# The first gather table made from the inputs, and the last wave's way back in three pieces with ScalarE and GpSimd

## The chip, the cores and the metric

The kernel runs on one core of a Trainium2 chip. Its time is device microseconds of one execution; the number that counts is the median of several. Times in the text are microseconds (us) unless marked ns. The engines are TensorE (PE, with its weight loads as PEld), VectorE (DVE), ScalarE (ACT), GpSimd (POOL) and SyncE (SP, which here only issues DMAs).

## What is computed

The input is a graph of 6250 nodes with 256 features and 106250 directed edges, sorted by target. One call runs two layers, each with graph sums, an attention without a softmax over pairs, and a feed-forward part:

```
xn = layernorm(x)
x  = x + gnn0(xn) + mix0(xn)          # two rounds of neighbour sums; linear attention
x  = x + ffn0(layernorm(x))           # each node goes to the one best of 8 experts
xn = layernorm(x)
x  = x + gnn1(xn) + mix1(xn)          # one round of neighbour sums
x  = x + ffn1(layernorm(x))           # 4 experts, top 2, and a shared part
```

A round of `gnn0` is `x + relu(D A D (x W) + b)`, where A is the adjacency and D the diagonal of 1/sqrt(deg) (`dinv` in the kernel). `gnn1` uses the mean over neighbours (`rdeg` is 1/max(deg, 1)).

## The kernel before

The nodes lie in 49 tiles of 128 rows, and `xa` holds all of them on chip as 128 x 49 x 256 fp32. The edges lie in 831 chunks of 128. A neighbour sum reads, for each chunk, 128 rows of a table in DRAM by an indirect DMA that GpSimd issues (L562), builds a 0/1 matrix of targets on VectorE (L566), and multiplies the two on TensorE into PSUM (L585). There are three such sums, with three tables: `t1` (fp32), `t2` and `t3` (each as fp32 and as three bf16 parts that add up to it; the sums read the parts). The stages in order:

1. Preparation: load the edges and `x`; count the degrees on TensorE (L414 to L435); the statistics of the first layer norm by `ln_stats` (L233, L234), `rstd` (square root on ScalarE L238, reciprocal on VectorE L239); the norm in place in `xa` on ScalarE (L469, groups of seven tiles); then `first_table` (L324): `dinv`, each tile times `dinv` alternately on ScalarE (L334) and VectorE (L336) into `t1s`, and a store of four tiles at a time into `t1` (L337).
2. The first sum over `t1`, and beside it the linear attention of `mix0` (`columns0`, L688: transposes of `xa`, then products), which settles tile by tile into `xa` and the table `t2`.
3. The second sum over `t2`; beside it the router of `ffn0` (`route`) sends nodes to slots of experts, and `serve` (L1056) takes slots in chunks of 128: 16 hidden products with Gelu on ScalarE (L915, L917), then the chosen expert's product (L1103). The nodes are two waves, tiles 0 to 35 and 36 to 48. When a wave is served, `back` (L1151) brings its rows home in pieces of two tiles.
4. The third sum over `t3` and beside it the attention and feed-forward of the second layer.

`back` of one piece: load `yb` (L1156); on VectorE add it to `xa` (L1160) and take statistics; square root on ScalarE; on VectorE the norm `xn` (L242); then `split` (L299) into three bf16 parts: a cast on ScalarE (L301), a subtraction on VectorE (L302), a cast (L303), a subtraction (L304); then both stores, `t3f` (L1172) and `t3b` (L1173). All first-wave pieces run while the second wave is served; the second wave's seven pieces (six of two tiles, one of one) run when no expert work is left, and the third sum needs all of `t3`.

What runs beside what is written by a planner, `pace` (L613). A job is a generator: each step issues instructions and yields the TensorE time it took and the time until its next step may go. `kinds` is a list of job sources by priority with the most that may live at once. In the stages of the sums the order of TensorE, SyncE and GpSimd is the order in which the planner issued; VectorE and ScalarE are ordered by the framework's scheduler. `later` puts an issue at a given time ahead in the planner's clock.

The lines that the change turns on:

```python
for T in range(t0, t0 + n):                                   # L469, in the preparation
    nc.scalar.activation(xa[:, T, :], xa[:, T, :], AF.Identity, bias=shift[...], scale=rs0[:, T:T + 1])
...
(lambda: backs, lambda: back(*backs.pop(0)), 2),              # two pieces alive at most
...
yield 0.0, 4.0 * n                                            # in back, between the work and the stores
```

Of the kernel before, what the change touches and what calls it, by code (L numbers as in the profile page):

```python
# [107 lines left out]
BT = 2  # L108
# [40 lines left out]
def gps_kernel(ctx: ExitStack, tc: tile.TileContext, i: dict, out: bass.AP):  # L149
# [73 lines left out]
    rdeg = consts.tile([P, NT], F32, name="rdeg")  # L223
    mv0 = consts.tile([P, NT, 2], F32, name="mv0")
    rs0 = consts.tile([P, NT], F32, name="rs0")
    mv1 = consts.tile([P, NT, 2], F32, name="mv1")
    rs1 = consts.tile([P, NT], F32, name="rs1")
    mv2 = consts.tile([P, NT, 2], F32, name="mv2")
# [67 lines left out]

    ov = dram.tile([NPAD, C], F32, name="ov")

    def split(dst, row, res):  # L299

        nc.scalar.copy(dst[:, :C], row)  # L301
        nc.vector.tensor_sub(res, row, dst[:, :C])  # L302
        nc.scalar.copy(dst[:, C:2 * C], res)  # L303
        nc.vector.tensor_sub(dst[:, 2 * C:], res, dst[:, C:2 * C])  # L304

    xa = nodes.tile([P, NT, C], F32, name="xa")
    sp = edges.tile([P, NCHP], I32, name="sp")
# [13 lines left out]

    gflag = consts.tile([1, 1], I32, name="gflag")

    def first_table(tp):  # L324

        sd = small.tile([P, NT], F32, name="sdeg")
        nc.scalar.activation(sd, deg, AF.Sqrt, bias=ones[:, 0:1], scale=1.0)
        nc.vector.reciprocal(dinv, sd)
        for t0, n in groups(4):
            ts = tp.tile([P, 4, C], F32, name="t1s", bufs=3)  # L330
            for t in range(n):
                T = t0 + t
                if t % 2:
                    nc.scalar.activation(ts[:, t, :], xa[:, T, :], AF.Copy, scale=dinv[:, T:T + 1])  # L334
                else:
                    nc.vector.tensor_scalar(ts[:, t, :], xa[:, T, :], dinv[:, T:T + 1], None, op0=ALU.mult)  # L336
            nc.sync.dma_start(tiles_of(t1[0], t0, n), ts[:, :n, :])  # L337
        dmx = small.tile([P, NT], F32, name="dmax")
        nc.vector.tensor_scalar(dmx, deg, 1.0, None, op0=ALU.max)
        nc.vector.reciprocal(rdeg, dmx)  # L340

    with ExitStack() as st:
        prep = pool(st, "prep")
# [114 lines left out]
        nc.vector.tensor_scalar(gpen, gpen, 1.0e6, None, op0=ALU.mult)  # L458
        nc.vector.tensor_scalar(lof, lof, gpen, None, op0=ALU.subtract)

        for t0, n in groups(7):
            for T in range(t0, t0 + n):
                ln_stats(mv0[:, T, :], xa[:, T, :])
            rstd(rs0[:, t0:t0 + n], mv0[:, t0:t0 + n, 1], n)
            shift = small.tile([P, 7], F32, name="shift")
            nc.vector.scalar_tensor_tensor(shift[:, :n], mv0[:, t0:t0 + n, 0], -1.0, rs0[:, t0:t0 + n],
                                           op0=ALU.mult, op1=ALU.mult)
            for T in range(t0, t0 + n):
                nc.scalar.activation(xa[:, T, :], xa[:, T, :], AF.Identity, bias=shift[:, T - t0:T - t0 + 1],  # L469
                                     scale=rs0[:, T:T + 1])  # L470
        first_table(pool(st, "table0"))

    general = nc.values_load(gflag[0:1, 0:1], min_val=0, max_val=1,
                             skip_runtime_bounds_check_because="it is the result of a comparison")
# [1 line left out]
    with tc.If(general):  # L476
        with ExitStack() as st:
            gw_ = pool(st, "gdeg")
            nc.vector.memset(deg, 0.0)
            hi = gw_.tile([P, NCHP], I32, name="g_hi")  # L480
            nc.vector.tensor_scalar(hi, dsti, 7, None, op0=ALU.arith_shift_right)
            hif = gw_.tile([P, NCHP], F32, name="g_hif")
            nc.vector.tensor_copy(hif, hi)
            nc.vector.tensor_scalar(hi, dsti, P - 1, None, op0=ALU.bitwise_and)
            low = gw_.tile([P, NCHP], F32, name="g_low")
            nc.vector.tensor_copy(low, hi)
            with tc.For_i(0, NCH, 1) as c:
# [10 lines left out]
                nc.vector.tensor_add(deg, deg, gd)  # L498
        with ExitStack() as st:
            first_table(pool(st, "table1"))  # L500

# [111 lines left out]
    def pace(kinds, slot, factor=1.0):  # L613

        now = [0.0]
        live = []

        def step():  # L620
            for k, (waiting, begin, most) in enumerate(kinds):
                while sum(j[1] == k for j in live) < most and waiting():
# [12 lines left out]

        def later(us, do):

            def once():
                do()
                yield from ()  # L640

            live.append([now[0] + us, None, once()])

        def due():

            for k, (waiting, begin, most) in enumerate(kinds):
                if sum(j[1] == k for j in live) < most and waiting():
# [12 lines left out]

        return step, other, rest, now, later
# [26 lines left out]
    def columns0():  # L688

        for gi, (t0, n) in enumerate(gs):  # L690
            transposed(xnt[:, :, t0 * P:(t0 + n) * P], lambda t: xa[:, t0 + t, :], n, "xtr", vs)
# [459 lines left out]
    def back(v, t0, n):  # L1151

        r = rows_of(t0 + n - 1)
        yb = work.tile([P, BT, C], F32, name="yb")
        y0 = 1 + (t0 - WAVES[v][0]) * P
        nc.sync.dma_start(yb[:r, :n, :], ys[v][y0:y0 + (n - 1) * P + r, :].rearrange("(t p) c -> p t c", p=r))  # L1156
# [7 lines left out]
        xn = work.tile([P, BT, C], F32, name="xn2")  # L1164
        ts = work.tile([P, BT, 3 * C], BF16, name="t3s")
        for t in range(n):
            T = t0 + t
            normalize(xn[:, t, :], xa[:, T, :], mv2[:, T, :], rs2[:, T:T + 1])
            res = work.tile([P, C], F32, name="res3")
            split(ts[:, t, :], xn[:, t, :], res)  # L1170
        yield 0.0, 4.0 * n
        nc.sync.dma_start(tiles_of(t3[0], t0, n), xn[:, :n, :])  # L1172
        nc.sync.dma_start(tiles_of(t3[1], t0, n), ts[:, :n, :])  # L1173

    def back_groups(v):

# [3 lines left out]
            yield v, t0, n  # L1180
            t0 += n

    routing, backs, finished = [], [], []

    filled = [v == len(WAVES) - 1 for v in range(len(WAVES))]
    waves, routed = list(range(len(WAVES))), [0]
# [30 lines left out]
    def serves():  # L1217
# [4 lines left out]
        if not filled[v]:  # L1222
# [1 line left out]
        finished.append(v)  # L1224

    step, other, rest, _, later = pace([(lambda: summed, lambda: settles(settle2), 1),
                                 (lambda: backs, lambda: back(*backs.pop(0)), 2),
                                 (lambda: routing, routes, 1),
                                 (lambda: waves and routed[0] > WAVES[waves[0]][0] + BEHIND, serves, 1)],
                                  1.25 * (NCH + NT + sum(map(chunks_of, range(len(WAVES))))) / NCH, factor=1.1)  # L1230
    with tc.manual_schedule(engines=ORDERED):
        neighbour_sums(t2, 1, gq, after2, True, other, depth=3)
        lag[:] = 1.0, 0.0
    gq_stack.close()
    for v in range(len(WAVES)):
# [444 lines left out]
```

## Time and profile before

| | |
|---|---|
| median of 3 runs | 3787.47 us (3784.19 to 3789.47) |
| the profiled execution | 3793.69 us, its span 3791.5 us |
| busy share of the span | PE 83%, PEld 68%, DVE 37%, ACT 26%, POOL 67% |
| first sum, first to last gather | 98.96 to 1173.88 us |
| second sum, first gather | 1192.12 us |
| last expert product ends | 2579.18 us |
| third sum, first gather | 2633.69 us |

An entry of a view names the source line, the engine, the operation, the tile written and the tile read, and the count; for a timeline the first two columns are start and length, and a bracket behind it says how long the engine had been idle and what ended that. A "waits" row reads: who waited, for what, us in total, times, longest. The framework's source lines of helpers (`ln_stats`, `rstd`, `split`) are shared by all callers, so tiles tell them apart.

### The profile page before, as it was taken

To read this page: it belongs to the slowest core of one execution; us is meant where nothing else is said; L and a number is where in the kernel's file an instruction comes from. 1 tells how busy PE (TensorE), PEld (TensorE's weight loads), DVE (VectorE), ACT (ScalarE), POOL (GpSimd) and SP (SyncE) were. 2 spreads that over 40 slices of the span, in tenths; PEclk is the share of its full clock that TensorE was granted. 3 is DMA by queue.
4 is the path that set the end of the run, shared out by engine and by line. 5 is a ranking of instruction groups with operands and counts; after the bars stand their busy time and mean duration, and the time that the engine had idled before them with its cause. 6 is when DMAs were issued, how large, how long until landed. Compare 5 with 4: busy or idle time off the path is not lost. (4 is left out here: it accounts for less than half of the span.)

```text
span 3791.5 us, 59772 instructions
## 1 busy us (share of the span) xinstructions
PE 3162.1 (83%) x23151; PEld 2579.1 (68%) x23151; DVE 1394.0 (37%) x5166; ACT 972.5 (26%) x2011; POOL 2536.0 (67%) x2657
## 2 busy tenths in 40 slices
PE   3788888878886778888888799873899999999998
PEld 2578777767774555666666576662788887778887
DVE  6222322222222223333333333563544445444444
ACT  4111100000000222333333242551123323233333
POOL 0777777777776777777777677312777777777772
PEclk9989866666665778999999899886999999999999
DMA  4566544444444556666666676585555555555552
GB/s 151 145 181 181 150 130 134 128 134 129 130 133 138 159 158 208 203 198 199 202 204 211 183 251 197 184 260 165 152 158 158 156 157 156 154 152 156 155 157 68
DMA packets 330381, 628.08 MB, mean 166 GB/s; under 512 B 56986, under 2 KB 219589, under 8 KB 330080
## 3 DMA queue, kind: packets, MB, share of 16 engines
q0 software_dynamic: 151488, 449.62, 40.8%
q1 hardware_dynamic: 177742, 174.07, 15.0%
q8 instruction: 184, 3.01, 0.3%
q14 instruction: 117, 0.96, 0.1%
q10 hardware_dynamic: 850, 0.43, 0.0%
HBM read 549.15 MB, written 74.75 MB: 165 GB/s over the span
## 5 line engine op out<-in xcount | busy, mean ns | idle before, releaser
L562 POOL DMA_INDIRECT rows<-t1f,sp x831 | 806.5, 971 | 358.4 <-issue 240.0
L562 POOL DMA_INDIRECT parts<-t3b,sp x831 | 808.4, 973 | 289.0 <-issue 214.2
L562 POOL DMA_INDIRECT parts<-t2b,sp x831 | 800.5, 963 | 290.0 <-issue 221.9
L585 PEld LDWEIGHTS <-parts 128*128 128x128 bf16 x9972 | 562.8, 103 | 432.3 <-DMA parts<-t2b,sp 209.0
L585 PE MATMUL sums<-onehotf,rows 128*128 128x84 f32 (+1 forms) x3324 | 660.9, 350 | 226.4 <-DMA rows<-t1f,sp 166.3
L585 PEld LDWEIGHTS sums<-onehotf,rows 128*128 128x128 f32 x3324 | 596.3, 255 | 321.5 <-DMA rows<-t1f,sp 224.6
L585 PE MATMUL sums<-onehot,parts 128*128 128x84 bf16 (+2 forms) x9972 | 659.9, 210 | 178.8 <-DMA parts<-t2b,sp 159.3
L915 PE MATMUL hid<-ft,fw 128*128 128x256 f32 (+1 forms) x1696 | 467.9, 411 | 21.3 <-DVE ft L275 8.6
L566 DVE TENSOR_TENSOR onehot<-iota_w,lof 128x336 bf16<-128x336 bf16 x416 | 209.6, 505 | 544.0 <-PE sums L585 483.5
L915 PEld LDWEIGHTS hid<-ft,fw 128*128 128x128 f32 x1696 | 311.2, 201 | 72.5 <-DVE ft L275 15.0
L566 DVE TENSOR_TENSOR onehotf<-iota_wf,lof 128x336 f32<-128x336 f32 x208 | 105.8, 509 | 548.3 <-PE sums L585 543.6
L917 ACT ACTIVATE ht<-hid,fb 128x256 f32<-128x256 f32 (+1 forms) x424 | 195.6, 472 | 259.1 <-PE hid L915 254.3
L1103 PE MATMUL exp<-wd,ht 128*128 128x256 f32 x896 | 229.6, 391 | 3.4 <-DMA wd<-in_L_ffn_Wd 3.1
L605 ACT COPY aggt<-sums 128x88 f32<-128x88 f32 x96 | 22.3, 232 | 737.5 <-PE sums L585 731.8
L1103 PEld LDWEIGHTS exp<-wd,ht 128*128 128x128 f32 x896 | 160.7, 192 | 21.2 <-DMA wd<-in_L_ffn_Wd 3.5
L1493 PE MATMUL fc_ps<-ht,fc 128*128 128x256 f32 (+1 forms) x600 | 160.6, 391 | 0.0
L1505 PE MATMUL fc_ps<-fc,ut 128*128 128x256 f32 x588 | 157.4, 393 | 0.0
L1075 POOL DMA_INDIRECT ys<-y,fs x56 | 56.7, 1012 | 134.4 <-DVE y L1108 64.4
L788 PE MATMUL h<-w,aggt 128*128 128x256 f32 x392 | 145.0, 507 | 0.3 <-DVE aggt L606 0.3
L936 PE MATMUL gate<-ht,wg 128*8 128x256 f32 (+1 forms) x400 | 112.5, 415 | 0.9 <-ACT ht L917 0.9
L1493 PEld LDWEIGHTS fc_ps<-ht,fc 128*128 128x128 f32 x600 | 105.0, 192 | 9.8
L1505 PEld LDWEIGHTS fc_ps<-fc,ut 128*128 128x128 f32 x588 | 102.9, 191 | 9.3
(358 smaller groups left out, 4145.1 us busy)
## 6 DMA issues: line engine op xcount, KB each, us to landing
wd<-in_L_ffn_Wd SPq DMA_DIRECT2D x56, 1024.0 KB
xs<-zero SPq DMA_DIRECT2D x8, 1799.0 KB
rows<-t1f,sp POOLq DMA_INDIRECT x831
parts<-t2b,sp POOLq DMA_INDIRECT x831
parts<-t3b,sp POOLq DMA_INDIRECT x831
t2b<-t2s SPq DMA_DIRECT2D x49, 192.0 KB
t3b<-t3s SPq DMA_DIRECT2D x24, 384.0 KB
fs<-xs SPq DMA_DIRECT2D x56, 128.5 KB
```

Source lines behind the costliest of these rows:

```text
L562: nc.gpsimd.indirect_dma_start(out=gs[:, j, :], out_offset=None, in_=(table if f32 else parts)[:, :], in_offset=bass.IndirectOffsetOnAxis( ...
L566: nc.vector.tensor_tensor(ohs[:, :n, :], (iota_wf if f32 else iota_w)[:, None, :WIN].to_broadcast([P, n, WIN]), lof[:, c:c + n, None].to_b ...
L585: nc.tensor.matmul(ps[b][:, h, n0 - b * P:n1 - b * P], lhsT=g[:, k * C + h * P:k * C + (h + 1) * P], rhs=oh[:, n0 - w0:n1 - w0], start=Fal ...
L605: nc.scalar.copy(dst[:, :, WIN:], sums[:, :, WIN:P])
L788: nc.tensor.matmul(h, lhsT=at[:, k, :], rhs=w[:, k, :], start=(k == 0), stop=(k == 1))
L915: nc.tensor.matmul(h_ps[:, :w], lhsT=fw1[:, k, m * P:(m + 1) * P], rhs=ft[:, k, :w], start=(k == 0), stop=(k == 1))
L917: nc.scalar.activation(ht[:, m, :w], h_ps[:, :w], AF.Gelu, bias=fb1[:, m:m + 1], scale=1.0)
L936: nc.tensor.matmul(lt, lhsT=wg[:, m, :], rhs=ht[:, m, :w], start=(m == 0), stop=(m == 7))
L1075: nc.gpsimd.indirect_dma_start(out=ys[v][:, :], out_offset=bass.IndirectOffsetOnAxis(ap=to, axis=0), in_=y, in_offset=None)
L1103: nc.tensor.matmul(y_ps, lhsT=ht[:, m, q * P:(q + 1) * P], rhs=wd[:, m, :], start=(m == 0), stop=(m == 7))
L1493: nc.tensor.matmul(u_ps[:, :w], lhsT=fc1[:, k, m * P:(m + 1) * P], rhs=ht[:, k, :w], start=(k == 0), stop=(k == 1))
L1505: nc.tensor.matmul(h_ps, lhsT=ut[:, m, t * P:(t + 1) * P], rhs=fc2[:, m, :], start=False, stop=(m == 5))
```

## The change

It has three parts.

The first table is made straight from the inputs. `dinv` and `rdeg` are taken in `factors`, as soon as the degrees are there. For groups of five tiles the norm's scale and shift are multiplied by `dinv` on VectorE (`by`), one ScalarE instruction per tile writes the table piece from the raw `xa`, and five tiles are stored at once. `xa` itself is normalised in place later, as a step of `columns0` in the first sum, on ScalarE, with a wait of 3 us in the planner's clock before the transposes. (The old form of `first_table` stays for a branch that these inputs do not take.)

The last wave's way back: up to three pieces alive (the bound of a kind may now be a function), the norm on ScalarE with a shift worked out on VectorE, the last subtraction of `split` on GpSimd. The first wave's pieces: one alive at a time. In both, a piece's job ends when its work is issued, and the stores are put `later`, 4 us per tile on in the planner's clock.

The tiles of `back` move from the pool `work` (two buffers) to a pool of their own, `backs` (three buffers), on the other side of the memory.

```diff
+    def factors():
         sd = small.tile([P, NT], F32, name="sdeg")
         nc.scalar.activation(sd, deg, AF.Sqrt, bias=ones[:, 0:1], scale=1.0)
         nc.vector.reciprocal(dinv, sd)
+        dmx = small.tile([P, NT], F32, name="dmax")
+        nc.vector.tensor_scalar(dmx, deg, 1.0, None, op0=ALU.max)
+        nc.vector.reciprocal(rdeg, dmx)
...
-        for t0, n in groups(7):
+        factors()
+        tp = pool(st, "table0")
+        for t0, n in groups(5):
             for T in range(t0, t0 + n):
                 ln_stats(mv0[:, T, :], xa[:, T, :])
...
-            for T in range(t0, t0 + n):
-                nc.scalar.activation(xa[:, T, :], xa[:, T, :], AF.Identity, bias=shift[:, T - t0:T - t0 + 1],
-                                     scale=rs0[:, T:T + 1])
-        first_table(pool(st, "table0"))
+            by = small.tile([P, 2, 5], F32, name="by", bufs=3)
+            nc.vector.tensor_mul(by[:, 0, :n], rs0[:, g], dinv[:, g])
+            nc.vector.tensor_mul(by[:, 1, :n], shift[:, g], dinv[:, g])
+            ts = tp.tile([P, 5, C], F32, name="t1s", bufs=3)
+            for t in range(n):
+                nc.scalar.activation(ts[:, t, :], xa[:, t0 + t, :], AF.Identity, bias=by[:, 1, t:t + 1],
+                                     scale=by[:, 0, t:t + 1])
+            nc.sync.dma_start(tiles_of(t1[0], t0, n), ts[:, :n, :])
...
     def columns0():
         for gi, (t0, n) in enumerate(gs):
+            for T in range(t0, t0 + n):
+                nc.scalar.activation(xa[:, T, :], xa[:, T, :], AF.Identity, bias=shift[:, T:T + 1],
+                                     scale=rs0[:, T:T + 1])
+            yield 0.0, 3.0
             transposed(xnt[:, :, t0 * P:(t0 + n) * P], lambda t: xa[:, t0 + t, :], n, "xtr", vs)
...
     def back(v, t0, n):
-        yb = work.tile([P, BT, C], F32, name="yb")
+        end = v == len(WAVES) - 1
+        yb = bk["pool"].tile([P, BT, C], F32, name="yb")
...
+            if end:
+                nc.scalar.activation(xn[:, t, :], xa[:, T, :], AF.Identity, bias=shift[:, t:t + 1],
+                                     scale=rs2[:, T:T + 1])
+            else:
+                normalize(xn[:, t, :], xa[:, T, :], mv2[:, T, :], rs2[:, T:T + 1])
+            split(ts[:, t, :], xn[:, t, :], res, nc.gpsimd if end else nc.vector)
-        yield 0.0, 4.0 * n
-        nc.sync.dma_start(tiles_of(t3[0], t0, n), xn[:, :n, :])
-        nc.sync.dma_start(tiles_of(t3[1], t0, n), ts[:, :n, :])
+        def store():
+            nc.sync.dma_start(tiles_of(t3[0], t0, n), xn[:, :n, :])
+            nc.sync.dma_start(tiles_of(t3[1], t0, n), ts[:, :n, :])
+        later(4.0 * n, store)
+        yield 0.0, 0.0 if end else 4.0
...
-                                 (lambda: backs, lambda: back(*backs.pop(0)), 2),
+                                 (lambda: backs, lambda: back(*backs.pop(0)), lambda: 3 if backs[0][0] else 1),
```

More of the change, by code (lines that the diff above doesn't have):

```diff
@@ L225, in gps_kernel @@
     rs0 = consts.tile([P, NT], F32, name="rs0")
+    shift = consts.tile([P, NT], F32, name="shift")
     mv1 = consts.tile([P, NT, 2], F32, name="mv1")
@@ L297, in gps_kernel, with split @@
     ov = dram.tile([NPAD, C], F32, name="ov")
-    def split(dst, row, res):
+    def split(dst, row, res, third=nc.vector):
         nc.scalar.copy(dst[:, :C], row)
@@ L303, in split @@
         nc.scalar.copy(dst[:, C:2 * C], res)
-        nc.vector.tensor_sub(dst[:, 2 * C:], res, dst[:, C:2 * C])
+        third.tensor_sub(dst[:, 2 * C:], res, dst[:, C:2 * C])
     xa = nodes.tile([P, NT, C], F32, name="xa")
@@ L322, in gps_kernel @@
     gflag = consts.tile([1, 1], I32, name="gflag")
-    def first_table(tp):
+    def factors():
         sd = small.tile([P, NT], F32, name="sdeg")
@@ L328, in first_table @@
         nc.vector.reciprocal(dinv, sd)
+        dmx = small.tile([P, NT], F32, name="dmax")
+        nc.vector.tensor_scalar(dmx, deg, 1.0, None, op0=ALU.max)
+        nc.vector.reciprocal(rdeg, dmx)
+    def first_table(tp):
         for t0, n in groups(4):
@@ L332, in first_table @@
                 T = t0 + t
[L333 to L336, printed above, removed]
+                nc.scalar.activation(ts[:, t, :], xa[:, T, :], AF.Identity, bias=shift[:, T:T + 1],
+                                     scale=rs0[:, T:T + 1])
+                nc.vector.tensor_scalar(ts[:, t, :], ts[:, t, :], dinv[:, T:T + 1], None, op0=ALU.mult)
             nc.sync.dma_start(tiles_of(t1[0], t0, n), ts[:, :n, :])
-        dmx = small.tile([P, NT], F32, name="dmax")
-        nc.vector.tensor_scalar(dmx, deg, 1.0, None, op0=ALU.max)
-        nc.vector.reciprocal(rdeg, dmx)
     with ExitStack() as st:
@@ L459, in gps_kernel @@
         nc.vector.tensor_scalar(lof, lof, gpen, None, op0=ALU.subtract)
-        for t0, n in groups(7):
+        factors()
+        tp = pool(st, "table0")
+        for t0, n in groups(5):
             for T in range(t0, t0 + n):
                 ln_stats(mv0[:, T, :], xa[:, T, :])
[L464 to L467, printed above, removed]
-            for T in range(t0, t0 + n):
-                nc.scalar.activation(xa[:, T, :], xa[:, T, :], AF.Identity, bias=shift[:, T - t0:T - t0 + 1],
-                                     scale=rs0[:, T:T + 1])
-        first_table(pool(st, "table0"))
+            g = slice(t0, t0 + n)
+            rstd(rs0[:, g], mv0[:, g, 1], n)
+            nc.vector.scalar_tensor_tensor(shift[:, g], mv0[:, g, 0], -1.0, rs0[:, g], op0=ALU.mult, op1=ALU.mult)
+            by = small.tile([P, 2, 5], F32, name="by", bufs=3)
[6 more added lines that the diff above has]
+            nc.sync.dma_start(tiles_of(t1[0], t0, n), ts[:, :n, :])
     general = nc.values_load(gflag[0:1, 0:1], min_val=0, max_val=1,
@@ L498, in gps_kernel @@
                 nc.vector.tensor_add(deg, deg, gd)
+        factors()
         with ExitStack() as st:
@@ L621, in step @@
             for k, (waiting, begin, most) in enumerate(kinds):
-                while sum(j[1] == k for j in live) < most and waiting():
+                while waiting() and sum(j[1] == k for j in live) < (most() if callable(most) else most):
                     live.append([now[0], k, begin()])
@@ L646, in due @@
             for k, (waiting, begin, most) in enumerate(kinds):
-                if sum(j[1] == k for j in live) < most and waiting():
+                if waiting() and sum(j[1] == k for j in live) < (most() if callable(most) else most):
                     return now[0]
@@ L690, in columns0 @@
         for gi, (t0, n) in enumerate(gs):
+            for T in range(t0, t0 + n):
+                nc.scalar.activation(xa[:, T, :], xa[:, T, :], AF.Identity, bias=shift[:, T:T + 1],
+                                     scale=rs0[:, T:T + 1])
+            yield 0.0, 3.0
             transposed(xnt[:, :, t0 * P:(t0 + n) * P], lambda t: xa[:, t0 + t, :], n, "xtr", vs)
@@ L1163, in back @@
         rstd(rs2[:, t0:t0 + n], mv2[:, t0:t0 + n, 1], n)
-        xn = work.tile([P, BT, C], F32, name="xn2")
-        ts = work.tile([P, BT, 3 * C], BF16, name="t3s")
+        if end:
+            shift = small.tile([P, BT], F32, name="shift2")
+            nc.vector.scalar_tensor_tensor(shift[:, :n], mv2[:, t0:t0 + n, 0], -1.0, rs2[:, t0:t0 + n],
+                                           op0=ALU.mult, op1=ALU.mult)
+        xn = bk["pool"].tile([P, BT, C], F32, name="xn2")
+        ts = bk["pool"].tile([P, BT, 3 * C], BF16, name="t3s")
         for t in range(n):
             T = t0 + t
-            normalize(xn[:, t, :], xa[:, T, :], mv2[:, T, :], rs2[:, T:T + 1])
-            res = work.tile([P, C], F32, name="res3")
-            split(ts[:, t, :], xn[:, t, :], res)
-        yield 0.0, 4.0 * n
-        nc.sync.dma_start(tiles_of(t3[0], t0, n), xn[:, :n, :])
-        nc.sync.dma_start(tiles_of(t3[1], t0, n), ts[:, :n, :])
+            if end:
+                nc.scalar.activation(xn[:, t, :], xa[:, T, :], AF.Identity, bias=shift[:, t:t + 1],
+                                     scale=rs2[:, T:T + 1])
+            else:
+                normalize(xn[:, t, :], xa[:, T, :], mv2[:, T, :], rs2[:, T:T + 1])
+            res = bk["pool"].tile([P, C], F32, name="res3")
+            split(ts[:, t, :], xn[:, t, :], res, nc.gpsimd if end else nc.vector)
[4 more added lines that the diff above has]
+        yield 0.0, 0.0 if end else 4.0
     def back_groups(v):
@@ L1181, in back_groups @@
             t0 += n
-    routing, backs, finished = [], [], []
+    routing, backs, finished, bk = [], [], [], {}
     filled = [v == len(WAVES) - 1 for v in range(len(WAVES))]
@@ L1234, in gps_kernel @@
     gq_stack.close()
+    bk["pool"] = pool(conv_stack, "backs", bufs=3)
     for v in range(len(WAVES)):
```

## The prediction

> **What bounds the kernel now.** I read the windows by stage first, then the timeline at the two places where TensorE stands still, then the waits of GpSimd in the first sum, then one stretch of the expert stage. The windows (columns: stretch, length, busy us of each engine, granted clock, DMA share, GB/s):
>
> ```profile
> core 0: us, PE busy (x) PEld busy (x) DVE busy (x) ACT busy (x) POOL busy (x), PEclk, DMA share, GB/s
> ...
> 75.00:100.00 25.00, 0.00 (x0) 0.00 (x0) 7.33 (x22) 10.82 (x25) 1.04 (x1) 1.00 0.77 253
> ...
> 2582.00:2642.00 60.00, 0.55 (x3) 0.18 (x4) 29.86 (x99) 11.45 (x33) 8.88 (x13) 0.51 0.47 157
> ...
> 2800.00:3300.00 500.00, 483.36 (x4044) 404.44 (x4044) 231.45 (x825) 155.12 (x301) 367.73 (x379) 0.98 0.55 156
> ```
>
> TensorE is the bound in the last sum (483 of 500 us). It does nothing at all in the preparation from 75 to 100 us, and 0.55 us between 2582 and 2642, the hand-over from the experts to the last sum. Whatever shortens these two stretches on every engine's chain moves all that follows. The timeline of the first stretch:
>
> ```profile
> 51.33 0.34 ACT L327 ACTIVATE sdeg<-deg,ones 128x49 f32<-128x49 f32 x1 [3.46 <-DVE deg L435]
> ...
> 66.63 0.43 DVE L328 RECIPROCAL dinv<-sdeg 128x49 f32<-128x49 f32 x1
> ...
> 71.84 0.89 ACT L334 ACTIVATE t1s<-xa,dinv 128x256 f32<-128x256 f32 x2
> ...
> 72.76 20.64 SPq L337 DMA_DIRECT2D t1f<-t1s  x13
> ...
> 92.67 0.35 DVE L336 TENSOR_SCALAR t1s<-xa,dinv 128x256 f32<-128x256 f32 x1 [1.11 <-DMA t1f<-t1s]
> ...
> 98.96 1.11 POOL L562 DMA_INDIRECT rows<-t1f,sp  x1 [89.03 <-DVE onehotf L566]
> ```
>
> The degrees are there at 51.3, but `dinv` is taken at 66.6, behind all statistics on VectorE, and ScalarE is busy with in-place norms until 71.65; only then do the table pieces `t1s` start. The last ends at 92.67 + 0.35 = 93.02, and the first gather starts 5.9 us later, when the table has landed. The second stretch, from SyncE and GpSimd:
>
> ```profile
> 2582.88 0.90 SPq L1156 DMA_DIRECT2D yb<-ys  x2
> ...
> 2594.10 1.30 SPq L1156 DMA_DIRECT2D yb<-ys  x2
> ...
> 2606.41 1.03 SPq L1156 DMA_DIRECT2D yb<-ys  x2
> ...
> 2618.62 0.31 SPq L1156 DMA_DIRECT2D yb<-ys  x1
> ...
> 2627.83 0.34 SPq L1173 DMA_DIRECT2D t3b<-t3s  x1
> ...
> 2633.69 1.68 POOL L562 DMA_INDIRECT parts<-t3b,sp  x1 [0.17 <-issue]
> ```
>
> Two pieces load at once and the next two only when both are stored: rounds of 11.2, 12.3 and 12.2 us and a single piece of 9.2, 44.95 us from first load to last store. Then 5.86 us to the first gather; the memsets of L1300 to L1348 take GpSimd from 2631.12 to 2633.52 of it.
>
> How a shift of the start is passed on is in the waits of GpSimd in the first sum:
>
> ```profile
> POOL rows L562 <- issue: 234.6, 760, 2.1
> POOL rows L562 <- DMA rows<-t1f,sp: 21.8, 28, 3.1
> ```
>
> 760 of 831 gathers wait only for their own queue: 0.95 + 0.30 = 1.25 us apart, 831 x 1.25 = 1039 of the 1076 us from 98.96 to 1174.8. The first sum is paced by GpSimd; TensorE's order in it is covered.
>
> Last, ScalarE between two hidden blocks of the expert stage:
>
> ```profile
> 2429.28 1.28 ACT L238 ACT_TABLE_LOAD   x1 [0.98 <-DVE mv L234]
> ...
> 2430.58 0.30 ACT L238 ACTIVATE sd<-mv,eps_t 128x2 f32<-128x2 f32 x1
> ...
> 2430.89 1.28 ACT L917 ACT_TABLE_LOAD   x1
> ...
> 2432.71 0.60 PE L936 MATMUL gate<-ht,wg 128*8 128x256 f32 x2 [0.94 <-ACT ht L917]
> ```
>
> A square root between two Gelus costs two table loads: from 2429.28 to the next Gelu at 2432.19 it is 2.91 us. TensorE lost 0.94 us by it, since the twenty hidden matmuls from 2423.96 had run ahead.
>
> **First table.** Removed from the preparation: 49 norms on ScalarE (17.6 us for 35, some 0.51 each where they run back to back, 3.55 / 7), 24 scalings there (0.45 each in pairs) and 25 on VectorE. Added: 49 norms that write the table, and twenty products of 128x5 on VectorE, at some 0.15 each like the shift of 128x7 (3 us, between statistics that take 0.39 a tile). `factors` now stands ahead, and in the built order `dinv` follows the square root of 51.33 at once; with the reciprocals (0.43 and 0.46) and the first products the first table norm starts at 53.7. ScalarE's order is 15 norms, 3 square roots, 15 norms, 4 square roots, 19 norms. 15 x 0.51 from 53.7 is 61.3; the roots and VectorE's answer to them cost 0.9; 15 more end at 69.8; VectorE has 12 tiles of statistics behind its own answer, so this second gap is 1.8; 19 more end at 81.3. Stores do not limit: the thirteen of before took from 72.76 to about 96 for the same bytes, and started at 56.3 that ends at 79.5. The last store is 4 tiles where it was one, which I put at 1 us. First gather: 81.3 + 5.9 + 1 = 88.2, a gain of 10.8 us. Bounds: 14 if the gaps vanish, 7 if the three buffers wait 4 us for stores.
>
> **Norms in the first sum.** 49 x 0.51 = 25 us of ScalarE, which was busy 1.76 of the 25 us from 100 to 125; and 13 waits of 3 us in the planner's clock, 39 us by which attention pieces move down TensorE's order. Both lie under the gathers' pace, so I take 0. If that cover goes, the price is a repeat of the buffer waits: 21.8 less the 28 x 0.3 that every gather waits, 13.4 us, of which 8 is my upper end; as the same waits may shrink, the lower end is -5.
>
> **First wave's pieces during the second wave's experts.** One at a time instead of two: 18 square roots now stand alone, and the next load no longer waits on SyncE for both pieces' stores. In the built order of ScalarE there are 33 table loads where there were 20, and 8 square roots inside a hidden block where there was one. 7 x 0.94 = 6.6 us for TensorE. Against it: with two pieces VectorE had 8.6 us of them at a stretch, and TensorE waited 6.0 us for VectorE's and 3.9 us for ScalarE's copies of `ft`; half of that, 5 us, should go. Net +2. Behind a waiting square root every Gelu is queued, and TensorE and SyncE's loads for the next pair wait for those; ends -8 (the 8.6 us wait for `fs` goes too) and +10. The Trainium skill (ScalarE: Activation LUTs, section "What ACT_TABLE_LOAD costs") puts a switch at 2.66 us with its drain. The row shows 1.28 and the root 0.02 us behind it; by the page each interruption would cost TensorE some 2.7 us more, 19 us in all, and the forecast would be 3779.
>
> **Last wave.** The per-tile work on VectorE before: update 0.44, statistics 0.39, norm 0.36, two subtractions 0.38 each. Norm and second subtraction leave it: 1.21 x 13 = 15.7, with reciprocal and shift 0.3 x 7 and one 0.47, 18.3 us. ScalarE: norm 0.51, two casts 0.72, 1.23 x 13 = 16.0, and 7 roots of 0.3, 18.1 us. GpSimd: 13 subtractions, for which the one row of that shape (bsum, L1332) has 0.74 (L373's 1.81 us for 833 columns would make it 0.56), 9.6 us, and 2.6 us of memsets now ahead of the branch. On SyncE the loads now stand ahead of the stores, and three buffers let them run: the fourth waits only for the first update. VectorE can start at 2585.7, ScalarE at 2587.6; 2587.6 + 18.1, the last subtraction and store 1.2, is 2607 if neither ever waits. Both are full and feed each other, so I add a fifth of the 18 us: 2610.5, against 2627.83, -17.3. The upper end is rounds as before, of three: 14 us (11.2 and one more piece's VectorE work) x 7/3 = 33, to 2616. Behind the last store the memsets no longer stand, -2.6, but weights of 768 KB are queued among the stores; at the 362 GB/s seen at 2640 that is 2.1 us, I take 1. Together -19, from -11 to -23.
>
> The Trainium skill (SBUF — State Buffer, section "Who interferes with whom") speaks against this part: VectorE and GpSimd share one port pair, locked for a whole instruction. Updates and first subtractions have two SBUF inputs, so by it up to 9.6 us would be added to VectorE's 18.3: 2585.7 + 27.9 + 1.2 is 2614.8, the tail would gain 14.6 and the total be 3764. No row here shows the two at once.
>
> **Sum.** -10.8 + 0 + 2 - 19 = -27.8. The profiled execution took 3793.69 (span 3791.5), so 3766; it lies 6.2 above the median of the runs, 3787.47, so 3760. A difference of 0.2%, 7.6 us, is about what a measurement of this kernel can tell from none.
>
> **Rivals.** (1) The tail gains least: VectorE and GpSimd hold each other up or pieces come in rounds; -11 for -19, so 3768. For it: both engines full. Chance 0.15. (2) The start is given back: attention, moved down 39 us, frees gather buffers late, +8 and 7 instead of 10.8; 3772. Against it: the first sum's pace above. Chance 0.1. (3) Slower: ScalarE's roots, put inside hidden blocks by the built order, wait there for a late load `yb` and hold every Gelu. Before, the root's longest wait for the statistics was 6.8 us, behind a block. If 8 roots wait 5 us each beyond the 0.94, that is 40 us against 30 from the other parts: 3797. It decides from 3.7 us on. Chance 0.08. The forecast itself has 0.67; its own range is 3748 to 3770.
>
> The range: full bounds are -14 -5 -8 -23 = -50 and -7 +8 +10 -11 = 0. All four at one end is unlikely; -42 to -9 takes in rivals 1 and 2 and leaves out 3 and the corners: 3745 to 3778. Faster by over 0.2%: the forecast, rivals 1 and 2, less a rest of 0.05: 0.87. Within: 0.06. Slower: 0.07.
>
> **What would show it.** First gather at 88 (84 to 92); `dinv` at 52; no scaling of `t1s` on VectorE. The first sum's gathers still 1.25 apart, ending 11 earlier. Between the waves' ends, TensorE's waits for `ht` up by 5 to 8 and for `ft` down. From the first `yb` of the second wave to the last store 27.6 us (24 to 33), first gather 4.3 behind. It is wrong if ScalarE's square roots wait for statistics inside hidden blocks, if GpSimd's subtraction takes over 1.5 us, or if the first sum ends no earlier.

## The result, and the profile after

| | before | after |
|---|---|---|
| median, six runs of each on one chip | 3788.27 us | 3760.26 us |
| ratio, 95% interval | | 0.9922 (0.9906 to 0.9937) |
| the profiled execution, its span | 3793.69, 3791.5 | 3761.78, 3760.0 |
| first gather of the first sum | 98.96 | 87.97 |
| first sum, first to last gather | 1074.9 | 1067.3 |
| second sum, first to last gather | 1206.3 | 1205.6 |
| from there to the last wave's first `yb` | 184.5 | 186.2 |
| from there to the last store | 44.95 | 31.04 |
| from there to the third sum's first gather | 5.86 | 6.35 |
| from there to the end | 1157.8 | 1156.1 |

Below, "experts" is the stretch from the last gather of the second sum to the last wave's first `yb`, "tail" the one from there to the last store, and "gap" the one from there to the third sum's first gather.

The changed kernel is 28 us faster, and the forecast, 3760, lies on the median. That is partly luck. Its terms do not all hold: in the profiled executions one that I had at nothing gave 7.6 us, and the largest fell 5.6 us short. And the spans of the two profiled executions differ by 31.5 us, since that of before lay 5.4 us above its median and that of after 1.5. Four of the kernels below (those with a first sum of some 1200 us) ran on a second chip, where every kernel, the one before too, takes 14% longer.

The windows of the changed kernel that answer to those of before (columns as there):

```profile
core 0: us, PE busy (x) PEld busy (x) DVE busy (x) ACT busy (x) POOL busy (x), PEclk, DMA share, GB/s
75.00:100.00 25.00, 4.95 (x23) 4.83 (x23) 2.22 (x6) 12.88 (x27) 9.29 (x10) 1.00 0.70 203
2566.51:2603.90 37.39, 0.51 (x1) 0.10 (x1) 20.07 (x71) 18.14 (x47) 10.63 (x19) 0.50 0.71 231
2588.00:2606.00 18.00, 0.51 (x1) 0.10 (x1) 6.36 (x22) 6.43 (x17) 7.35 (x14) 0.50 0.90 284
```

The hand-over from experts to third sum now takes 37.4 us of which VectorE is busy 20.1, ScalarE 18.1 and GpSimd 10.6. None of them is full. The DMA engines have a share of 0.71 over the whole of it, where before they had 0.39 (2582.88 to 2633.69), and of 0.90 from 2588 to 2606.

The timeline of the start (start, length, engine, line, operation; in the bracket how long the engine had stood idle and for what):

```profile
53.15 0.34 ACT L328 ACTIVATE sdeg<-deg,ones 128x49 f32<-128x49 f32 x1 [33.67 <-DVE deg L438]
...
53.97 0.44 DVE L329 RECIPROCAL dinv<-sdeg 128x49 f32<-128x49 f32 x1
...
55.44 7.48 ACT L479 ACTIVATE t1s<-xa,by 128x256 f32<-128x256 f32 x15 [1.95 <-DVE by L476]
...
58.03 24.07 SPq L481 DMA_DIRECT2D t1f<-t1s  x10
...
72.26 9.44 ACT L479 ACTIVATE t1s<-xa,by 128x256 f32<-128x256 f32 x19 [0.15 <-DVE by L476]
...
87.97 1.11 POOL L573 DMA_INDIRECT rows<-t1f,sp  x1 [78.05 <-DMA w<-in_L_gnn_W]
```

`dinv` is taken right behind the square root, the 49 table norms run from 55.44 to 81.70 with two short gaps, and the ten stores keep up with them. Here little is left to gain but the 6.3 us from the last norm to the first gather. The waits of GpSimd in the first sum:

```profile
POOL rows L573 <- issue: 238.5, 779, 1.5
...
POOL rows L573 <- DMA rows<-t1f,sp: 18.2, 31, 2.8
```

The same view of the kernel before, over its whole first sum (the row in the prediction, with 760 waits, is that of 100 to 1150 us):

```profile
POOL rows L562 <- issue: 240.0, 778, 2.1
```

Of these rows only the waits for gathered rows changed much, from 21.8 to 18.2.

ScalarE and TensorE in one hidden block, while the first wave's pieces come home:

```profile
2501.48 1.28 ACT L239 ACT_TABLE_LOAD   x1
2502.77 0.29 ACT L239 ACTIVATE sd<-mv,eps_t 128x2 f32<-128x2 f32 x1
2503.09 1.28 ACT L932 ACT_TABLE_LOAD   x1
...
2504.91 1.13 PE L930 MATMUL hid<-ft,fw 128*128 128x256 f32 x4 [1.37 <-ACT ht L932]
...
2505.47 1.28 ACT L239 ACT_TABLE_LOAD   x1
...
2507.68 1.28 ACT L932 ACT_TABLE_LOAD   x1
...
2509.50 4.78 PE L930 MATMUL hid<-ft,fw 128*128 128x256 f32 x11 [3.46 <-ACT ht L932]
```

Two square roots stand in one block of Gelus. Each costs two table loads, and TensorE waits 1.37 and then 3.46 us for `ht`. In the whole stretch there are seven such waits, of 0.74 to 3.46 us, 14.1 us together, where before there were three of 1.6 us together. TensorE's waits in this stretch, after and then before:

```profile
PE hid L930 <- ACT ht L932: 8.2, 4, 3.5
PE hid L930 <- DVE ft L276: 7.1, 8, 1.6
PE exp L1118 <- ACT ht L932: 6.0, 3, 2.4
```

```profile
PE ftr L269 <- DMA fs<-xs: 8.6, 1, 8.6
PE hid L915 <- DVE ft L275: 6.0, 8, 1.7
PE hid L915 <- ACT ft L273: 3.9, 2, 2.3
```

All its waits there, the smaller ones too, come to 28.1 us after and 29.1 before. Last, the hand-over:

```profile
2566.51 5.76 SPq L1173 DMA_DIRECT2D yb<-ys  x5
...
2571.59 1.28 ACT L239 ACT_TABLE_LOAD   x1 [11.94 <-DVE mv L235]
...
2574.72 3.58 SPq L1173 DMA_DIRECT2D yb<-ys  x2
...
2576.21 1.76 DVE L1177 SCALAR_TENSOR_TENSOR xa<-yb,pbest,xa 128x256 f32<-128x256 f32 x2
...
2576.21 1.48 POOL L305 TENSOR_TENSOR t3s<-res,t3s 128x256 bf16<-128x256 f32 x2 [11.71 <-ACT t3s L304]
...
2578.34 0.39 SPq L1198 DMA_DIRECT2D t3f<-xn  x1
...
2584.46 0.60 ACT L1190 ACTIVATE xn<-xa,shift,rs 128x256 f32<-128x256 f32 x1 [2.12 <-DMA t3f<-xn]
...
2597.55 0.54 SPq L1199 DMA_DIRECT2D t3b<-t3s  x1
...
2603.90 1.26 POOL L573 DMA_INDIRECT parts<-t3b,sp  x1 [7.26 <-DMA t3b<-t3s]
```

Four things are to be seen. The first table load waits for the statistics together with its square root, and so its 1.28 us lie on the path. Two updates on VectorE take 1.76 us beside GpSimd's subtractions, where two take 0.88 in run 9, which has none on GpSimd. The first piece's `t3f` is issued only at 2578.34, behind loads that wait on SyncE for free `yb` buffers; its buffer comes free 6 us later, and ScalarE waits 2.12 us for that. And the last store lands some 6 us after its issue.

### The profile page after: what moved, and what is told of

It reads as the page before. It is cut to its first block, busy times and chain, and to the rows that moved or that the text cites. A ratio compares the mean times of both kernels' runs of the same rounds, so it can differ in the third digit from the quotient of the medians.

```text
span 3760.0 us, 59818 instructions
## 1 busy us (share of the span) xinstructions
PE 3148.6 (84%) x23151; PEld 2573.0 (68%) x23151; DVE 1383.5 (37%) x5148; ACT 1006.3 (27%) x2065; POOL 2540.7 (68%) x2670
## 5 line engine op out<-in xcount | busy, mean ns | idle before, releaser
L596 PE MATMUL sums<-onehotf,rows 128*128 128x84 f32 (+1 forms) x3324 | 647.9, 347 | 223.4 <-DMA rows<-t1f,sp 177.1
L596 PEld LDWEIGHTS sums<-onehotf,rows 128*128 128x128 f32 x3324 | 587.0, 253 | 313.0 <-DMA rows<-t1f,sp 228.9
```

Source lines behind the costliest of these rows:

```text
L596: nc.tensor.matmul(ps[b][:, h, n0 - b * P:n1 - b * P], lhsT=g[:, k * C + h * P:k * C + (h + 1) * P], rhs=oh[:, n0 - w0:n1 - w0], start=Fal ...
```

## The experiments

My theory after the first reading: the gain is the start (11), a shorter first sum because attention stands later in TensorE's order (7.6) and the tail (13.4 with the gap behind it), less 1.7 in the expert stage. Rival one: the 7.6 us are chance. Rival two: the tail falls short of the forecast because VectorE and GpSimd hold each other up, not because of the DMA queue.

### 1 and 2. Each half alone

`e1_table_only` is the changed kernel with the pieces as before:

```diff
-        yb = bk["pool"].tile([P, BT, C], F32, name="yb")
+        yb = work.tile([P, BT, C], F32, name="yb")
...
-        later(4.0 * n, store)
-        yield 0.0, 0.0 if end else 4.0
+        yield 0.0, 4.0 * n
+        # both stores here
...
-        (lambda: backs, lambda: back(*backs.pop(0)), lambda: 3 if backs[0][0] else 1),
+        (lambda: backs, lambda: back(*backs.pop(0)), 2),
```

> The changed kernel with the pieces of both waves as they were (two at a time, stores ahead of the next load, all on VectorE and ScalarE's casts): the first table and the in-place norms in the first sum alone. Theory: the gain consists of the start (11.0 us), of a first sum that is 7.7 us shorter because attention stands later and frees gather buffers at better times, and of the tail, less 1.7 in the expert stage. Then here the first gather is at 88, the first sum (first to last gather) takes 1067, the tail takes 45 us from first yb to last store, and the time is 18 below before, 3770. Rival one (the 7.7 us are an accident of the profiled execution of before or after): the first sum takes 1075 and the time is 11 below, 3777.

`e2_back_only` is the kernel before with `split`, `back`, the kinds and the pool of the changed one (the second half of the diff).

> The kernel before with the pieces of the change alone: last wave three at a time with ScalarE and GpSimd, first wave one at a time; start and first sum untouched, so that its first sum is also a second look at that of before. Theory: first gather at 99, first sum 1075 again, expert stage 1.7 us longer than before (TensorE's waits for ht 14 us where there was 1), first yb to last store 31 us, first gather of the last sum 6.3 behind it, in all 13 below before: 3775. Rival one (accident): the first sum lies anywhere from 1067 to 1075. If the first wave's pieces are worth more or less than the 1.7 that I read out of two traces, the time from the last gather of the second sum to the first yb of the second wave tells it: 184 here, 183 before.

| | time | ratio to before | first gather | first sum | experts | tail | gap |
|---|---|---|---|---|---|---|---|
| e1, table only | 3772.74 | 0.9959 (0.9946 to 0.9973) | 87.50 | 1069.7 | 183.8 | 44.87 | 4.67 |
| e2, pieces only | 3772.74 | 0.9964 (0.9953 to 0.9975) | 98.19 | 1070.3 | 184.9 | 30.34 | 7.50 |

Of the 3788.5 us that the kernel before took beside them, the table is worth 15.5 us (10 to 20) and the pieces 13.6 (10 to 18). Together that is the 29 of the whole, so within these intervals the halves do not disturb each other. For run 1 theory had a first sum of 1067 and 3770, rival one 1075 and 3777: it lies between them. The start alone explains 11.5 of the first 15.5. But e2, whose first sum is that of before, needs 1070.3 for it where theory had 1075: so some 4.6 of the 7.6 us may be the one execution of before that was profiled.

### 3. The last subtraction on VectorE

```diff
-            split(ts[:, t, :], xn[:, t, :], res, nc.gpsimd if end else nc.vector)
+            split(ts[:, t, :], xn[:, t, :], res)
```

> The changed kernel with the last subtraction of the split on VectorE in both waves, GpSimd taking no part. Theory: GpSimd's subtraction relieves VectorE by 13 x 0.38 = 4.9 us and costs it about 2.7 us by running at the same time, so first yb to last store grows from 31 to about 33, the time by 2. Rival two (the tail falls short of the forecast because VectorE and GpSimd hold each other up): the tail is as short or shorter without GpSimd, 29 to 31, and the longest update falls from 0.97 back to 0.45.

3759.75 us, 0.9928 (0.9906 to 0.9950): no different from the changed kernel. The tail of this kernel:

```profile
2565.66 5.58 SPq L1173 DMA_DIRECT2D yb<-ys  x5
...
2575.96 0.46 DVE L1177 SCALAR_TENSOR_TENSOR xa<-yb,pbest,xa 128x256 f32<-128x256 f32 x1
...
2595.42 0.49 SPq L1199 DMA_DIRECT2D t3b<-t3s  x1
```

From 2565.66 to 2595.42 it is 29.76 us, and no update takes longer than 0.48. My theory, which expected 33, is wrong, and rival two fits: what GpSimd takes off VectorE it gives back by slowing it, and in the changed kernel its subtraction takes 0.64 to 0.76 us where VectorE's takes 0.38. How much that is worth one tail does not tell. In five executions with the changed kernel's hand-over (the changed kernel twice, runs 2, 6 and 10) the tail was 29.97 to 31.04 and the gap 5.50 to 8.33, a long one mostly with a short other, and both together 36.4 to 38.4. Here they are 35.0 together, 1.4 below the lowest of these.

### 4. The weights behind the stores

```diff
+    lw = pool(ctx, "l1late")
-    ws = wl.tile([P, 2, C], F32, name="ws")
+    ws = lw.tile([P, 2, C], F32, name="ws")
     # the same for the layer's other weights; two memsets from GpSimd to VectorE
```

> The changed kernel with the weights of the last sum's layer in a pool that is opened behind the stores, so that their loads (2.1 MB) no longer stand between the stores of the last wave on SyncE; two memsets move from GpSimd to VectorE. Theory: the DMA engines, 89% busy from 2588 to 2606 in the changed kernel, are what made the last store land 5 us after its issue and the third piece's buffer come late; without the weights the share falls to under 60%, the last store lands within 3 us, the last sum's first gather is 3.5 to 4.5 behind the last store instead of 6.3, first yb to last store is 1 to 3 shorter, and the time is 3 to 6 below the changed kernel. Rival two (the engines set the tail, not the DMA queue): the gap from last store to first gather falls by under 1 and the time is the same; it may be longer if TensorE then waits for weights at the start of the last sum's first columns.

3759.50 us, 0.9929 (0.9910 to 0.9948). The two windows of its hand-over:

```profile
2571.65:2592.00 20.35, 0.00 (x0) 0.00 (x0) 15.49 (x54) 10.96 (x28) 4.11 (x6) 0.50 0.58 192
2592.00:2606.81 14.81, 0.51 (x1) 0.10 (x1) 5.08 (x18) 7.07 (x21) 6.06 (x12) 0.50 0.53 186
```

The DMA share of the second half falls from 0.90 to 0.53. The gap behind the last store falls from 6.35 to 4.53, about the upper end of what the theory had. But the tail itself stays at 30.63, and ScalarE still waits 2.1 us for a store of `xn`: the weights held up the last store's landing, not the stores before it. That is 2 us where 3 to 6 were expected, too little to see in the time.

### 5. First wave two at a time

```diff
-   (lambda: backs, lambda: back(*backs.pop(0)), lambda: 3 if backs[0][0] else 1),
+   (lambda: backs, lambda: back(*backs.pop(0)), lambda: 3 if backs[0][0] else 2),
```

> The changed kernel with the first wave's pieces two at a time again (the last wave's stay at three). Runs so far: from the last gather of the second sum to the first yb of the second wave it is 184.5 and 183.8 with two at a time, 186.2, 184.9, 185.0 and 186.1 with one. Theory: square roots stand again in pairs behind the hidden blocks, TensorE's waits for ht in that stretch fall from 14 us to under 2, its waits for fs, wd and ft come back, and the stretch takes 184, the time 1 to 2 less than the changed kernel. Rival: it is the order of loads and stores (the next load no longer behind both stores, as the change has it in both) that took the wait for fs away, and then two at a time keeps that as well and the stretch takes 178 to 180.

Both are wrong. On the second chip the stretch takes 198.9 us, where the changed kernel's arrangement has 185.2 and 185.4 there (runs 6 and 7) and before 182.8. TensorE's longest wait in it:

```profile
2826.49 0.37 SPq L1199 DMA_DIRECT2D t3b<-t3s  x1
...
2833.34 0.15 DVE L1049 CAST pi<-pf 1x2 int32<-1x2 f32 x1
...
2834.04 2.31 SPq L1059 DMA_DIRECT2D fs<-xs  x2
...
2836.15 0.44 PE L270 MATMUL ftr<-ident,fs 128*128 128x128 f32 x1 [16.59 <-DMA fs<-xs]
```

The next chunk is chosen by a chain of tiny instructions on VectorE, the last of them L1049. With two pieces alive VectorE works on pieces from 2816 to 2833, the choice is late, and so are the load `fs` and TensorE: 16.6 us. The 8.6 us wait for `fs` of the kernel before is in part a wait of this kind: there the choice came at 2487.54, late behind pieces, and the load went out at 2491.01, behind a store and two loads on SyncE. With one piece at a time it is gone: on the first chip it is 8.2 us in run 1 and 0.3 in run 2. That about pays for the table loads. The tail is 27.4 and the gap 3.07 here, with the first wave already home: all seven loads go out in 8.8 us ahead of every store, and the table load is off the path. Time: 0.9962 (0.9945 to 0.9979).

### 6. Without the planned time for the norms

```diff
-            yield 0.0, 3.0
+            yield 0.0, 0.0
             transposed(xnt[:, :, t0 * P:(t0 + n) * P], lambda t: xa[:, t0 + t, :], n, "xtr", vs)
```

> The changed kernel without the 3 us that the planner gives each group of in-place norms, so attention's matmuls stand in TensorE's order about where they stood before. First to last gather of the first sum so far: 1074.9 and 1070.3 where the norms are in the preparation, 1067.3, 1069.7, 1067.8 and 1070.3 where they are in the first sum. Theory: the 4 us between the means come from attention standing 39 us later in the order, so here it is 1071 to 1075, and the time 3 to 6 above the changed kernel. Rival one (chance of the execution, or of the start, and not the order): 1067 to 1071, and no difference in time. Rival four (TensorE now waits for norms that have no planned time): above 1075.

Nothing can be read from this run: on the second chip the first sum takes 1199.5 here and 1198.2 in run 5, and 1200.1 in the kernel before, which was run again there.

> The kernel before once more, for a third look at its first sum. Theory: 1070 to 1075 from first to last gather, mean of the three above 1071. Rival one: 1067 to 1070, so that the two kinds cannot be told apart.

Its waits of GpSimd in the first sum show why:

```profile
POOL rows L562 <- issue: 221.6, 727, 0.4
POOL rows L562 <- remote: 134.0, 58, 3.8
```

A kind of wait that the first chip does not show at all, "remote" (it ended by nothing that this core's profile shows), takes 134 us in 58 stretches. The waits for gathered rows, in which the difference was sought, are 4.9 us there. GpSimd's own pace is the same on both chips: the median distance of two gathers in the kernel before is 1.25 us on each. The mean is 1.30 us on the first and 1.45 on the second, and these waits, not GpSimd alone, make most of that difference. So it was run again as run 10, beside the changed kernel itself, and this time on the faster chip.

> The changed kernel without the 3 us of the planner for each group of norms, beside the changed kernel on one chip. In the earlier run the gathers were 1.45 us apart, GpSimd alone set the pace, and the first sum (1199.5) told nothing. Theory (the place of attention in the order makes the 4 us): where gathers are 1.31 apart, first sum 1071 to 1075 and 3 to 6 above the changed kernel. Rival one (chance of the execution): within 2 us of it in both.

> The changed kernel once more, as the measure for the three that run beside it, and for a fifth look at its first sum. Theory: 28 below before where the gathers are 1.31 us apart, first sum 1067 to 1071 there; where they are 1.45 apart, as they were for the last four kernels, first sum 1198 to 1205 as for the kernel before, and only the start and the tail are gained, 24. Tail 31 from first yb to last store, first gather 6 behind.

The changed kernel took 3756.77 us, 0.9932 (0.9919 to 0.9945), with a first sum of 1064.5, a tail of 30.94 and a gap of 5.50. Without the planned time it took 3761.13, 0.9935 (0.9921 to 0.9949), with a first sum of 1073.0, a tail of 29.97 and a gap of 7.76. On the faster chip there are now three first sums with the norms in the preparation or without planned time (1074.9, 1070.3, 1073.0) and seven with it (1063.4 to 1070.3, mean 1066.8). That speaks for the theory, at some 6 us. It does not settle it: the two ratios are the same within their intervals, and the profiled execution with 1073.0 was the slowest of its kernel's six. Nor do the runs made side by side agree: in runs 1 to 4 it is 1070.3 without for 1067.8 to 1070.3 with planned time, in runs 8 to 10 1073.0 for 1063.4 to 1064.5.

### 7. Three mends at once

Late weights, the subtraction on VectorE, and besides:

```diff
-        yb = bk["pool"].tile([P, BT, C], F32, name="yb")
+        yb = bk["pool"].tile([P, BT, C], F32, name="yb", bufs=2)
...
+        if end and t0 == WAVES[v][0]:
+            ahead = small.tile([P, 1], F32, name="ahead")
+            nc.scalar.activation(ahead, yb[:, 0, 0:1], AF.Sqrt, bias=eps_t, scale=0.0)
...
-        xn = bk["pool"].tile([P, BT, C], F32, name="xn2")
+        xn = bk["pool"].tile([P, BT, C], F32, name="xn2", bufs=4)
```

> The version that the runs point to: the changed kernel with the late weights, the last subtraction on VectorE, four buffers for xn2 (two for yb) in place of three of each, and a square root of one element behind the first yb load, so that the table load no longer waits for the statistics. From first yb to last store it was 31.0 in the changed kernel, 29.8 with the subtraction on VectorE, 30.6 with the late weights; from there to the first gather 6.3, 5.3 and 4.5. Theory (each of the four is on the path): 29.8 less 1.3 for the table load and 1 to 1.7 for ScalarE's wait for the store of xn, so 27, and then 4.5: 31.5 for 37.4, a time 6 below the changed kernel. Rival five (the tail is now bounded by VectorE's and ScalarE's work feeding each other, and a wait taken away is found again at the next one): 29 and 4.5, a time 3 to 4 below.

Tail 29.6, gap 4.6 on the second chip (0.9963, 0.9946 to 0.9981): rival five. The table load did leave the path, but with two `yb` buffers SyncE's loads wait longer, the stores behind them go out later, and ScalarE's wait for a store of `xn` grew from 2.1 to 4.0 us.

### 8. The stores sooner

```diff
-        later(4.0 * n, store)
+        later((1.0 if end else 4.0) * n, store)
```

> The changed kernel, with the planner's delay of a last-wave store 1.0 n instead of 4.0 n: on SyncE the seventh load, which waits for an update of VectorE to free its buffer, then stands behind the stores of the first three pieces and not ahead of them. Theory (SyncE's order makes ScalarE's wait for xn: in the changed kernel the first piece's norm was done at 2574.8, its store was issued at 2578.3, behind that load, landed 6 us later, and ScalarE waited 2.1 us for it): first store 3 us sooner, ScalarE's wait for t3f gone or under 0.5, first yb to last store 29 for 31, time 2 below. Rival five (it is the work of VectorE, ScalarE and GpSimd that bounds it): the wait goes and comes back as waits for one another, the tail stays at 30.5 to 31.5. It may grow if the seventh load now comes late for VectorE.

3755.36 us, 0.9925 (0.9910 to 0.9941), beside the changed kernel's 3756.77: no difference. SyncE, VectorE and ScalarE:

```profile
2568.11 0.46 SPq L1198 DMA_DIRECT2D t3f<-xn  x1
...
2578.69 0.31 SPq L1173 DMA_DIRECT2D yb<-ys  x1
...
2584.27 0.48 DVE L1177 SCALAR_TENSOR_TENSOR xa<-yb,pbest,xa 106x256 f32<-106x256 f32 x1 [2.54 <-DMA yb<-ys]
...
2585.46 0.29 ACT L239 ACTIVATE sd<-mv,eps_t 128x1 f32<-128x1 f32 x1 [2.38 <-DVE mv L235]
```

The first store goes out at 2568.11, 8.6 us after the first load where it was 11.8, and no norm of ScalarE waits for a store any more. But now the last load stands behind stores. It is issued at 2578.69, VectorE waits 2.54 us for it and ScalarE 2.38 for VectorE. The tail is 31.67, just above what rival five had. SyncE's order was the cause of the wait, as the theory says, and taking the wait away brought another, as rival five says. The gap is 3.00, since most of the weights come behind the last store in this order, and so tail and gap together are 34.7 for the changed kernel's 36.4.

### 9. The version that the runs point to

Late weights, the subtraction on VectorE, the early square root and the stores sooner, with three buffers each.

> Late weights, last subtraction on VectorE, the one-element square root ahead of the statistics, and the stores sooner, with three buffers each as in the changed kernel. With two yb buffers the fifth norm waited 4.0 us for a store that stood behind a load on SyncE, and the tail was 29.6 and 4.6. Theory: without that wait 29.6 less 3 to 4, so 26, then 4.5: 30.5 where the changed kernel has 37.4, and 6 to 7 below it in time. Rival five: 28 to 29, and 4 below.

3746.82 us, 0.9908 (0.9893 to 0.9922), where the changed kernel beside it took 3756.77. It is the fastest of all (its interval just touches that of the changed kernel), but the tail (29.54) and the gap (3.89) explain only 3.0 of the 10 us; 2.9 more lie in the expert stage, which the edits do not touch and which took 184.9 to 190.8 in the other profiled executions of the first chip with one piece at a time. The other 4 us are not explained. Why the tail is no shorter:

```profile
2553.87 5.64 SPq L1173 DMA_DIRECT2D yb<-ys  x5
...
2556.67 0.88 DVE L1180 SCALAR_TENSOR_TENSOR xa<-yb,pbest,xa 128x256 f32<-128x256 f32 x2 [1.90 <-DMA yb<-ys]
...
2570.02 0.35 SPq L1173 DMA_DIRECT2D yb<-ys  x1
...
2576.17 0.48 DVE L1180 SCALAR_TENSOR_TENSOR xa<-yb,pbest,xa 106x256 f32<-106x256 f32 x1 [3.85 <-DMA yb<-ys]
...
2577.47 0.74 ACT L304 CAST t3s<-res 128x256 bf16<-128x256 f32 x2 [3.33 <-DVE res L303]
```

The last load, of one tile, takes 6.15 us from issue to the first instruction that uses it. The first load, of two tiles, took 2.80 with no store beside it. VectorE takes up the last tile's update before the subtractions of the fifth piece, and stands 3.85 us, ScalarE 3.33.

## Why the prediction was right, and where it was not

**Start: -10.8 forecast, -11.0 measured.** The degrees came 1.8 us later than before (53.15), the second gap was 0.9 where I had 1.8, and the last norm ended at 81.70 where I had 81.3. The bounds held.

**Norms in the first sum: 0 forecast, -7.6 measured, outside the lower end of -5.** The step that missed is "Both lie under the gathers' pace, so I take 0". The norms did stay covered; what the step left out is that the sum could get shorter. In the profiles of the faster chip the mean over seven executions with the planned time is 1066.8, and 1072.6 over two with the norms in the preparation (before and run 2), so some 6 of the 7.6 us may be an effect; the rest may be chance. Waits for gathered rows explain about half of it (18 for 21 in the mean, but 23.6 in run 1). That the later place of attention does it is made likely by run 10, and not shown: the cause stays open.

**First wave's pieces: +2 forecast, +1.7 measured, and the agreement is luck.** Each of the seven pauses that reached TensorE cost it 2.0 us in the mean, not 0.94; the longest, 3.46, is one where a second square root stands in the same block. That made +12.5 in place of 6.6. Against it the wait for `fs` went (-7.8), which I had only at the lower end, and with it 2.8 us of waits for `ft` and 3.1 for `wd`. With the small ones TensorE's waits fell by 1.0 us; the stretch is 1.7 longer because the rest of it, TensorE's own work, took 2.7 more. That rest was 155.4 before, and 155.0 to 159.4 in the first chip's executions with one piece at a time, so the 1.7 is not told from chance. Runs 1 and 2 show that the wait for `fs` goes with the change of the pieces, and run 5 that it stays with two at a time. The price of 2.66 us for a switch of tables in the Trainium skill (ScalarE: Activation LUTs, "What ACT_TABLE_LOAD costs") is not borne out here: the load takes 1.28, the root starts 0.01 to 0.02 behind it, and from 2501.48 to the next Gelu at 2504.38 it is 2.90 for two loads and the root.

**Last wave: -19 forecast with the gap, -13.4 measured.** The term that was mis-sized is "a fifth of the 18 us" for two engines that feed each other: 3.6 us, where by the same sum 7 were lost: the tail took 31.0 for 27.6. The runs show parts of it: the table load, which had no term (1.3, off the path in runs 7 and 9), GpSimd beside VectorE (1.3 of tail in run 3, within the scatter of tails; 1.4 or more of tail and gap together), SyncE's order of loads and stores (2.1, run 8). They do not add up: run 9 has all three mends and gains 1.4 us of tail. The gap was to be 4.3 and is 6.35. Without the memsets, 2.6, that of before would be 3.3, so the weights cost some 3 where I had 1: in the trace 1280 KB of them (`ws`, `wn` and the first `fc`) go out ahead of the last store, where the sum had 768. Run 4 takes 1 to 2 us of that away. What the Trainium skill says (SBUF — State Buffer, "Who interferes with whom"), which I set against this part, was right in kind: a VectorE update beside a GpSimd subtraction takes up to 0.97 us where it takes 0.48 at most in run 3, and handing the subtraction to GpSimd gained nothing. Of the 9.6 us that could be lost by it, VectorE lost some 2.5: its updates took 7.7 us for 6.1 in run 3, its first subtractions 6.0 for 5.5 and its shifts 1.3 for 1.0.

**What had no term.** From the last gather of the first sum to the first of the second it is 1.3 us longer, the second sum 0.7 and the third stage 1.7 shorter. The third stage has scattered from 1152.0 to 1160.0 on this chip, so none of this is read as an effect.

**Rivals.** Rival 1 of the forecast (the tail gains least, -11 for -19, 3768) was nearer than the forecast in the tail, at -13.4. Its 3768 did not come, because the first sum, a term that I had at nothing, was shorter by about as much. Rival 2 had the first sum's sign wrong. Rival 3 (square roots that wait for late `yb` inside hidden blocks) did not come: the pauses are table loads, 2.0 us each in the mean and 3.46 at most, under the 3.7 from which it decides.

## What to carry to other kernels

When a wait on a queue that is served in order is taken away, ask which instruction the queue holds next: here the mends of runs 7 to 9 moved the 2 us wait to another buffer, and the sum of single gains was never reached. When two neighbouring stretches trade time, as the tail and the gap do here, compare their sum, over several executions. Small control work on an engine that also does bulk work (the choice of the next chunk behind the pieces on VectorE) can cost the bound engine more than any table load. And a term of a sum that is set to nothing because "another engine sets the pace" should keep a few us of range on both sides, since between profiled executions of kernels with the same first sum it alone moved by 5 to 7.

## What I had not expected of the hardware

- A transfer on SyncE's queue took 2.8 us from issue to use with no store beside it (a load of 256 KB, run 9) and 5.6 to 6.2 when stores were under way (106 KB loads of runs 8 and 9, a 256 KB store of the changed kernel), at a DMA share of only 0.63 to 0.74.
- On the second chip the same program spent 134 us of the first sum in "remote" waits of GpSimd that the first chip does not show, and took 14% longer. The three variants that ran there (runs 5 to 7) had ratios to the kernel before of 0.9945 to 0.9963; the changed kernel itself was not run there.
